# A two-layer transformer kernel: the gate products behind the last latent scores, q by ScalarE, the last expert chunks by bank, and a transpose behind the first attention step

## The chip, the core and the metric

The kernel runs on one core of one Trainium2 chip. A core has a matrix engine (TensorE, in the profile PE, with its weight loads as PEld), a vector engine (VectorE, DVE), an activation engine (ScalarE, ACT), GpSimd (POOL) and SyncE (SP), which here issues the DMAs. Each engine works through its own queue in order, and the queues meet at semaphores. Matrix products land in PSUM, which the kernel divides into eight banks; VectorE or ScalarE must read a bank before TensorE may fill it again.

The metric is the device time of one execution in microseconds (us), the median of several runs. Lower is better.

## The reference

The input is 1,024 tokens of 256 features (one sequence; B = 1). Two layers follow, each an attention and an expert stage, with a layer norm that is scaled and shifted ("modulated") ahead of each and a gated residual behind it:

```python
mod = (silu(L0_c) @ L0_wmod).reshape(1, 6, 1, -1)          # sa, ca, ga, sb, cb, gb
ga = (2 * (ga >= 0) - 1) * maximum(abs(ga), 0.25)           # gb the same
h = layernorm(x) * (1 + ca) + sa
x = x + ga * L0_attn(h)     # 16 heads with a low-rank latent (64 wide), rotary part; and a small
                            # "pattern" attention of 16 heads, 16 wide; mixed by a softmax gate
h = layernorm(x) * (1 + cb) + sb
x = x + gb * L0_ffn(h)      # 8 experts of 256: silu(h Wg) * (h Wu), down by Wd, weighted per token
mod = (silu(L1_c) @ L1_wmod).reshape(1, 6, 1, -1)
h = layernorm(x) * (1 + ca) + sa
x = x + ga * L1_attn(h)     # 16 heads, 16 wide, biases, causal, a slope per head on the key's place
h = layernorm(x) * (1 + cb) + sb
x = x + gb * L1_ffn(h)      # u + 2 shared + 16 routed experts of 176, relu, the top 4 of a sigmoid
return x
```

In the second layer's attention q = h Wq + bq, k = h Wk + bk, and the scores are q k / sqrt(16) plus slope times place, masked above the diagonal. In its expert stage the hidden units of all experts are laid side by side: 25 chunks of 128 units.

## The kernel before

**Tiling.** Tokens lie in tiles of 128 partitions, in two halves of 512 tokens (`i` = 0, 1), each half with its own `x`, `acc` and transposed features `hT`. All data are 32-bit floats. PSUM is cut into three kinds of tile by `sc_tile` and `mm_tile`: two "sc" tiles of two banks (128 x 1024), two "nn" banks and two "mm" banks (128 x 512). `mm_tile()` hands out nn and mm in turn. A tile is handed out again only after the engine that reads it is done; that is the commonest wait of TensorE here.

**Order of the work.** In most stages TensorE's order is that of the program text (`manual_schedule`); the order on VectorE, ScalarE and GpSimd is partly left to a scheduler when the kernel is built. Where the text interleaves two strands, one is a Python generator that is moved on at planned points of the other: `plan`/`side` in the second half, `at(n, ...)` in the latent attention.

**Latent attention of layer 0** (lines 860 to 1065). 128 tiles `n` of scores: 16 units `u` of eight (a head pair and a half of the tokens), `n = 8u ... 8u+7`. In iteration `n` the loop does `scores(n + 2)`: two products of 512 columns into an sc tile (L706), a row maximum on VectorE (`nmax`, L710, 128x1024), an exponential on ScalarE (`pr`, L914). Then `transposed(n)`: a block transpose of the probabilities on VectorE (`pt`, L923). Then whatever `at(n, ...)` put there: for unit `u`, `by_latent` (L938, a transpose of one over the sums) at `8u+8`, the products of probabilities and latents, `over_latents`, in two parts at `8u+9` and `8u+11` (L955, 128 small matmuls each, into four nn/mm banks, which ScalarE (L967) and VectorE (L970, eight additions) read at the end of the second part, and GpSimd multiplies at L972), and four `out_part` (L977, read by VectorE at L978) at `8u+14` to `8u+16`.

Also put there are two sets of products that belong to the next layer's modulation. `by_rows(1, 1, ...)` at `last - 12` = 116: two products of 512 columns (four matmul records, L126) into an mm/nn bank, which ScalarE copies out (L128, L131). `by_columns(1, 0, ...)` at `last - 4` = 124: eight products of one column (16 records, L111), which VectorE copies out (`modT`, L116 and L119). Here `last` = 128 is the first index behind the loop. Behind the loop, in the order of `n`: the last out parts of unit 14 (L977, at 128), the residual and layer norm of the first half on VectorE (L183, L184, L160 to L172; at 128), `over_latents(15, 0)` at 129, `by_latent(15)` and `over_latents(15, 1)` at 131, the transposes of the first half's features (`by_feature`, L196) at 132.

**Experts of layer 0** (L1191, L1169). The first pieces of the second layer are moved in between: the first half's projections of head pair 0 and the first eight score items (`firsts`).

**Attention of layer 1** (`small_attention`, lines 254 to 450). A projection gives k (`put_k`, L1232, ScalarE, with scale and bias; then DMAs that write the slope row into k, L1238) and q (`put_q`, L1225, VectorE), two instructions of 128x512 each. `step(i)` does one key tile of four heads' second scores (L337, into nn/mm banks; exponentials on ScalarE, L347) and, beside them, one or two first-score items (`first`, L299 into sc tiles, mask products L356, row maxima on VectorE, L305). Ahead of the loop stand the residual and layer norm of the second half (VectorE), the rest of the first half's projections and values (`rest`: L243, L250; values are copied out by ScalarE L67 and VectorE L69 in turn), and `by_feature(1, 0, 1)`, eight transposes (L196) with two ScalarE copies (L204). In the loop, `plan[0]` to `plan[4]` move on `parts`, the second half's projections: k and q of pair 0 after step 0, of pair 1 after step 1, two value tiles after step 2 and two after step 3. `plan[19]` starts `output` (transposes of the attention result, L463), `plan[21]` ends it.

**Experts of layer 1** (`modulated_experts`, lines 1293 to 1341). For each of the 25 chunks `c`: `hidden(c)` (L1307, ReLU on ScalarE L1308, times a gate row on VectorE L1316), then `down(c - 2)` (L1323), which adds the chunk into two accumulating banks: tokens 0 to 255 of the half in bank 0, 256 to 511 in bank 1. After the last chunk VectorE multiplies each bank by the gate (L1339), adds x (L1340), and SP sends 256 tokens to the output (L1341); bank 0 first.

Of the kernel before, what the change touches and what calls it, by code (L numbers as in the profile page):

```python
# [10 lines left out]
AF = mybir.ActivationFunctionType  # L11
ALU = mybir.AluOpType
AX = mybir.AxisListType

P = 128
T = 1024
NT = T // P
HID = 256
# [19 lines left out]
NC1 = -(-OWNED[-1][2] // P)  # L38
# [4 lines left out]
def adaln_two_layers(ctx: ExitStack, tc: tile.TileContext, a: dict, out: bass.AP):  # L43
    nc = tc.nc
# [7 lines left out]
    sc_tile = lambda: psum.tile([P, T], F32, tag="sc", name="sc")  # L52
# [51 lines left out]
    def by_columns(l, i, w, bank):  # L104

        js = ((0, 1, 2, 3), (6, 7), (8, 9))[i]
        pm = bank()
        for j in js:
            at = j * P - 512 * i
            for k in range(2):  # L110
                nc.tensor.matmul(  # L111
                    pm[:, j : j + 1], w[k][:, at : at + P], cs[:, 2 * l + k : 2 * l + k + 1],
                    start=(k == 0), stop=(k == 1),
                )
        if i < 2:
            nc.vector.tensor_copy(modT[l][:, 6 * i : 6 * i + 2], pm[:, 6 * i : 6 * i + 2])  # L116
        if i != 1:
            at = 2 + 3 * i
            nc.vector.tensor_scalar_add(modT[l][:, at : at + 2], pm[:, at : at + 2], 1.0)  # L119

    def by_rows(l, i, w, bank):

        ps = bank()
        cols = slice(0, 512) if l else slice((i - 1) * HID, i * HID)
        for k in range(2):
            nc.tensor.matmul(ps[:, cols], crep[l][:, k, :], w[k][:, cols], start=(k == 0), stop=(k == 1))  # L126
        gate = slice((i - 1) * HID, i * HID)
        nc.scalar.copy(gates_bc[l][:, gate], ps[:, gate])  # L128
        if l == 1:
            by_token[i] = base.tile([P, HID], F32, tag=f"bc{i}", name="bc")  # L130
            nc.scalar.copy(by_token[i], ps[:, (2 - i) * HID : (3 - i) * HID])  # L131
# [54 lines left out]
    def by_feature(l, which, i, double=False):  # L186

        done = which is None
        if double:
            sc = sc_tile()  # L190
            pts = [sc[:, :512], sc[:, 512:]]
        else:
            pts = [mm_tile() for _ in range(2)]
        for t in range(4):
            for k in range(2):
                nc.tensor.transpose(  # L196
                    pts[k][:, t * P : (t + 1) * P], acc[i][:, t, k * P : (k + 1) * P], ident
                )
        for k in range(2):
            if done:  # L200
                evacuate(hT[i][:, k, :], pts[k])
            else:
                s0 = 6 * which + k
                nc.scalar.activation(  # L204
                    hT[i][:, k, :], pts[k], AF.Identity,
                    bias=modT[l][:, s0 : s0 + 1], scale=modT[l][:, s0 + 2 : s0 + 3],
                )
# [279 lines left out]
    with pool("l0a") as l0, pool("mla") as ml:  # L487
# [10 lines left out]
        scale = (DN + DR) ** -0.5  # L498
# [390 lines left out]
        with pool("mla1") as m1, pool("mla2", 2) as m2:  # L889
# [96 lines left out]
            def at(n, fn, *args):  # L986
                beside.setdefault(n, []).append((fn, args))
# [44 lines left out]
            at(110, weights_of_thirds)  # L1032
            at(112, reload)
            last = 8 * len(units)
            at(last - 12, lambda: by_rows(1, 1, thirds[1], mm_tile))
            at(last - 4, lambda: by_columns(1, 0, thirds[0], mm_tile))
            at(last, residual, 0, gates_bc[0][:, :HID])
            at(last, lambda: whole(normalized(0)))
            at(last + 4, by_feature, 0, 1, 0, True)
# [182 lines left out]
    alibi = a["alibi"].rearrange("(g j) t -> j g t", j=4)  # L1222

    def put_q(dst, g, i, ps):
        nc.vector.tensor_scalar(  # L1225
            dst[:, g, i * 512 : (i + 1) * 512], ps, own4[:, g % 2 : g % 2 + 1], bias[:, 0, g : g + 1],
            ALU.mult, ALU.add,
        )

    def put_k(dst, g, i, ps):  # L1230
# [63 lines left out]
    def modulated_experts(i, tag, bank):  # L1294


        sums = [mm_tile(tag) for _ in range(2)]
        chunks = {}

        def hidden(c):  # L1300
            w = load(a["moe_w"][c].rearrange("p (b m) -> p b m", b=2))
            w1 = w[:, 0, :].rearrange("p (k m) -> p k m", k=2)
            if c % 2 == 0:
                chunks["he"] = he_tile()
            ps, he = bank[0](), chunks["he"][:, c % 2, :]
            for k in range(2):
                nc.tensor.matmul(ps, w1[:, k, :], hT[i][:, k, :], start=(k == 0), stop=(k == 1))  # L1307
            nc.scalar.activation(he, ps, AF.Relu, bias=b1[:, c : c + 1])  # L1308
            rows = [(n, r0, r1) for n, r0, r1 in OWNED if r0 < (c + 1) * P and r1 > c * P]
            if len(rows) > 1 or rows[0][0] != NE1:  # L1310
                g = row_tile()
                for n, r0, r1 in rows:
                    p0, p1 = max(r0 - c * P, 0), min(r1 - c * P, P)
                    by = gate_rows[i][n, :].partition_broadcast(p1 - p0) if n is not None else gate_rows[i][:NE1, :]
                    nc.sync.dma_start(g[p0:p1, :], by)
                nc.vector.tensor_mul(he, he, g)  # L1316
            chunks[c] = (he, w[:, 1, :])

        def down(c):
            he, w2 = chunks.pop(c)  # L1320
            for t in range(4):

                nc.tensor.matmul(  # L1323
                    sums[t // 2][:, t % 2 * HID : (t % 2 + 1) * HID], he[:, t * P : (t + 1) * P], w2,
                    start=(c == 0 and t % 2 == 0), stop=(c == NC1 - 1 and t % 2 == 1),
                )

        for c in range(NC1 + 2):
            if c < NC1:
                hidden(c)  # L1330
                yield
            if c > 1:
                down(c - 2)
                yield
        ov = out.rearrange("o (t p) d -> p (o t) d", p=P)
        for b in range(2):
            for t in (2 * b, 2 * b + 1):
                at = tmp.tile([P, HID], F32, name="at")
                nc.vector.tensor_mul(at, sums[b][:, t % 2 * HID : (t % 2 + 1) * HID], gates_bc[1][:, HID:])  # L1339
                nc.vector.tensor_add(x[i][:, t, :], x[i][:, t, :], at)  # L1340
            nc.sync.dma_start(ov[:, 4 * i + 2 * b : 4 * i + 2 * b + 2, :], x[i][:, 2 * b : 2 * b + 2, :])  # L1341
# [24 lines left out]
    with tc.manual_schedule(engines={mybir.EngineType.PE}):  # L1366
        wts = [golden(0, spare[0]), None]

        def later():
            wts[1] = golden(1)  # L1370
            gates(1, lambda: row_tile()[:, :HID])

        do = side({5: [(lambda: by_feature(0, 1, 1), None)], 8: [(later, None)]})
        for n, _ in enumerate(golden_experts(0, wts[0], True)):
            do(n)
        residual(0, gates_bc[0][:, HID:])
        whole(normalized(0))
        gated_output()

        qT, kT, v = small_tensors(l1)  # L1380
        nrm = l1.tile([P, 4, NH, 16], F32, name="nrm")
        late = [l1, [nrm, nrm]]
        firsts, step, n_steps, last_divided = small_attention(l1, qT, kT, v, True, late)
        next(firsts)
        parts = projections(0, [0], False)
        plan = {2: [(parts, 1)], 4: [(lambda: by_feature(1, 0, 0), None)]}
        for n in range(2):
            plan[6 + n] = [(parts, 1)]
        for n in range(8):
            plan[9 + 2 * n] = [(firsts, 1)]  # L1390
        do = side(plan)
        for n, _ in enumerate(golden_experts(1, wts[1], False)):
            do(n)
            if n == 20:
                rest = projections(0, [1], True)
                next(rest)
        residual(1, gates_bc[0][:, HID:])
        whole(normalized(1))
        whole(rest)
        parts = projections(1, [0, 1], True)  # L1400
        next(parts)
        by_feature(1, 0, 1)

        output = small_output(in_two(he_tile()), nrm, wo, put, 0, bv, (ones, bo))
        inputs = experts_input(0, nc.gpsimd)
        plan = {n: [(parts, 2)] for n in range(5)}
        plan[19], plan[21] = [(output, 1)], [(output, 2)]
        for n in range(4):
            plan[22 + n] = [(inputs, 1)]
        plan[26] = [(inputs, 1)]  # L1410
        plan[31] = [(inputs, 1)]
        for n in range(33, 39):
            plan[n] = [(inputs, 1)]
        plan[40] = [(inputs, 1)]
        do = side(plan)
        bank, half = [mm_tile], [None]

        def beside_experts(n):
            step(n)
            do(n)  # L1420
            if n == 37:
                singles[:] = ["mm", "mm"]
                half[0] = modulated_experts(0, "nn", bank)
            if n >= 38:
                next(half[0])

        for n in range(30):
            beside_experts(n)
# [143 lines left out]
```

## Time and profile before

| | |
|---|---|
| median of three runs | 1320.95 us (1320.94, 1320.95, 1322.4) |
| time of the profiled execution | 1324.29 us |
| its span, first to last instruction | 1322.5 us |
| mean granted TensorE clock in it | 0.996 |
| PE, PEld busy | 1284.1 us (97%), 691.8 us (52%) |
| DVE, ACT, POOL busy | 835.9 us (63%), 619.6 us (47%), 244.4 us (18%) |

Times in a profile are in us from the start of the span. A row of the timeline gives start, length, engine, source line, operation, what is written from what, and shape; in square brackets the idle time of that engine just before, and whose work ended it. The list of waits gives, for one engine, what waited for whom, with total, number and longest. The view by stretches gives the busy time of the engine in a stretch, and the clock that it was granted (1.00 is full speed). Matmul ends are modelled, and a product of 32-bit floats appears as two records.

### The profile page before, as it was taken

What the parts mean: (1) busy time and instruction counts of PE and PEld (TensorE: products, weight loads), DVE (VectorE), ACT (ScalarE), POOL (GpSimd) and SP (SyncE); (2) the same over time, 40 slices, a digit from 0 to 9 for tenths busy, and PEclk for the clock granted to TensorE, in tenths of its full rate; (3) what the DMA queues carried; (4) which work ended last, traced back from release to release, by engine and by line L of the source; (5) the groups of instructions that cost most, each with busy time, mean ns of one, the idle gap of its engine ahead of it and who ended that gap; (6) DMA issues with size and microseconds to landing.
All of it is one profiled execution on the core that took longest, in us unless ns stands there. A gap on an engine that the chain in (4) does not pass through costs nothing.

```text
span 1322.5 us, 25183 instructions
## 1 busy us (share of the span) xinstructions
PE 1284.1 (97%) x10588; PEld 691.8 (52%) x10588; DVE 835.9 (63%) x1290; ACT 619.6 (47%) x1153; POOL 244.4 (18%) x241
## 2 busy tenths in 40 slices
PE   9999999999999999999999899999989999999998
PEld 6533234324555555555555566655656454566665
DVE  4678877737787787887878875344566675152222
ACT  5366665565756657575665333111045565312121
POOL 5000000042535335252543010000000040020000
PEclk9999999999999999999999999999999999999999
DMA  9100000000000000000004022222210000325441
GB/s 285 51 0 1 1 1 1 1 1 17 10 5 6 6 5 10 2 9 2 2 1 160 2 56 71 80 80 72 65 42 10 2 2 3 112 92 162 148 157 48
DMA packets 56666, 58.82 MB, mean 44 GB/s; under 512 B 15143, under 2 KB 42280, under 8 KB 56554
## 3 DMA queue, kind: packets, MB, share of 16 engines
q1 hardware_dynamic: 56010, 57.22, 14.4%
q8 instruction: 83, 1.36, 0.4%
q14 instruction: 29, 0.24, 0.1%
q10 hardware_dynamic: 544, 0.00, 0.0%
HBM read 55.05 MB, written 1.12 MB: 42 GB/s over the span
## 4 chain that ended last, share of the span: by engine, by line
PE 89%; DVE 7%; issue 1%; POOL 1%; ACT 1%; DMA 0%; DVEq 0%; ACTq 0%; POOLq 0%
PE sc L706 17%; PE sc L299 11%; PE sc L1307 6%; PE mm L955 5%; DVE mx L305 4%; PE sc L1191 4%; PE nn L955 4%; PE nn L369 4%; PE nn L1323 3%; PE mm L1323 3%; PE mm L369 3%; PE nn L1169 2%; PE nn L1191 2%; PE mm L1169 2%; PE mm L1191 2%; PE mm L666 2%
## 5 line engine op out<-in xcount | busy, mean ns | idle before, releaser
L305 DVE TENSOR_REDUCE mx<-sc 128x2 f32<-128x1024 f32 (+3 forms) x224 | 239.6, 1106 | 51.9 <-PE sc L299 15.6
L299 PE MATMUL sc<-kT,qT 32*128 32x512 f32 (+3 forms) x896 | 204.8, 585 | 18.7 <-DVE mx L305 18.4
L914 ACT ACTIVATE pr<-sc,nmax 128x1024 f32<-128x1024 f32 x128 | 142.5, 1113 | 168.9 <-DVE nmax L710 163.0
L337 PE MATMUL nn<-q,kT 32*128 32x512 f32 (+3 forms) x384 | 189.0, 590 | 2.0 <-DVE t L626 2.0
L337 PE MATMUL mm<-q,kT 32*128 32x512 f32 (+3 forms) x384 | 187.2, 593 | 0.5 <-DVE qf L671 0.5
L923 DVE STREAM_TRANSPOSE pt<-pr 128x1024 f32<-128x1024 f32 x128 | 157.3, 1236 | 42.2 <-ACT pr L914 42.0
L710 DVE TENSOR_REDUCE nmax<-sc 128x1 f32<-128x1024 f32 x128 | 154.3, 1214 | 43.5 <-PE sc L706 41.7
L347 ACT ACTIVATE pt<-nn 128x512 f32<-128x512 f32 (+1 forms) x192 | 106.8, 556 | 62.9 <-PE mm L337 42.8
L347 ACT ACTIVATE pt<-mm 128x512 f32<-128x512 f32 (+1 forms) x192 | 106.9, 557 | 55.9 <-PE nn L337 23.4
L955 PE MATMUL mm<-pt,kv 32*64 32x256 f32 x2048 | 124.9, 382 | 2.4 <-DVE pt L923 2.4
L955 PE MATMUL nn<-pt,kv 32*64 32x256 f32 x2048 | 122.5, 382 | 0.7 <-ACT bc L942 0.7
L706 PE MATMUL sc<-kf,qf 128*128 128x512 f32 x256 | 121.1, 604 | 1.5 <-ACT pr L914 1.2
L706 PE MATMUL sc<-x,qf 128*128 128x512 f32 x256 | 121.0, 604 | 1.2 <-ACT pr L914 1.1
L299 PEld LDWEIGHTS sc<-kT,qT 32*128 32x128 f32 x896 | 65.9, 184 | 102.7 <-DVE mx L305 87.5
L1316 DVE TENSOR_TENSOR he<-he,row 128x512 f32<-128x512 f32 x46 | 31.7, 692 | 128.5 <-ACT he L1308 106.8
L635 POOL TENSOR_TENSOR t<-t,cos 128x512 f32<-128x512 f32 x32 | 40.7, 1272 | 350.3 <-PE sc L337 217.4
L955 PEld LDWEIGHTS nn<-pt,kv 32*64 32x64 f32 x2048 | 87.5, 133 | 18.2 <-DVE acc L978 6.4
L955 PEld LDWEIGHTS mm<-pt,kv 32*64 32x64 f32 x2048 | 85.0, 133 | 23.0 <-issue 5.5
L1308 ACT ACTIVATE he<-sc,b 128x512 f32<-128x512 f32 x43 | 29.5, 687 | 123.3 <-PE sc L1307 123.3
L1307 PE MATMUL sc<-hT,w 128*128 128x512 f32 x172 | 80.7, 593 | 0.0
L706 PEld LDWEIGHTS sc<-x,qf 128*128 128x128 f32 x256 | 45.6, 190 | 57.7 <-issue 51.4
L706 PEld LDWEIGHTS sc<-kf,qf 128*128 128x128 f32 x256 | 45.5, 190 | 56.7 <-issue 51.9
(382 smaller groups left out, 2117.0 us busy)
## 6 DMA issues: line engine op xcount, KB each, us to landing
w<-in_moe_w_dram SPq DMA_DIRECT2D x50, 256.0 KB
w<-in_wg_dram SPq DMA_DIRECT2D x16, 256.0 KB
w<-in_wu_dram SPq DMA_DIRECT2D x16, 256.0 KB
w<-in_wd_dram SPq DMA_DIRECT2D x16, 256.0 KB
row<-gD SPq DMA_DIRECT2D x14, 256.0 KB
x<-in_x_dram SPq DMA_DIRECT2D x4, 512.0 KB
wo<-in_o_dram SPq DMA_DIRECT2D x1, 2048.0 KB
wm<-in_wmod_dram SPq DMA_DIRECT2D x6, 256.0 KB
```

The lines of the kernel that those rows point to most:

```text
L299: nc.tensor.matmul(sc[:, i, :n], qT[r, g, qt * P : (qt + 1) * P], kT[r, g, c * 512 : c * 512 + n], start=True, stop=not diag,)
L305: nc.vector.tensor_reduce(mx[:, qi, c, 2 * pair : 2 * pair + 2], sc[:, :, :n], AX.X, ALU.max)
L337: nc.tensor.matmul(ps[:, q0:], kT[r, g, kc * P : (kc + 1) * P], state[u]["q2"][r, q0:], start=True, stop=not diag,)
L347: nc.scalar.activation(pt[:, 2 * pair + i, q0:], ps[:, q0:], AF.Exp)
L369: nc.tensor.matmul(av[PW * j : PW * (j + 1), q0:], v[:, kc, 4 * g + j, :], pt[:, j, q0:], start=(n == some[0]), stop=(n == some[-1]),)
L706: nc.tensor.matmul(sc[:, c], qfs[p, i][j][:, t * P : (t + 1) * P], kf[p % 2][j][:, c], start=True, stop=True)
L710: nc.vector.tensor_reduce(nmax, sc, AX.X, ALU.max, negate=True)
L914: nc.scalar.activation(pr, sc, AF.Exp, bias=nmax, accum_out=sums[u][:, t, j : j + 1])
L923: nc.vector.transpose(pts[u][:, :, slice(1, 3) if j else slice(0, 4, 3), 32 * t : 32 * t + 32], prs.pop(n).rearrange("p (b c k) -> p b c k ...
L955: nc.tensor.matmul(av[r][64 * c : 64 * c + 64, : 2 * P], kv32[row, b + c, :], pt[row, b // 2, 2 * c : 2 * c + 2, :].rearrange("p j q -> p ...
L1191: nc.tensor.matmul(gu[s], w[s][:, k, f * P : (f + 1) * P], hT[i][:, k, :], start=(k == 0), stop=(k == 1),)
L1307: nc.tensor.matmul(ps, w1[:, k, :], hT[i][:, k, :], start=(k == 0), stop=(k == 1))
```

## The change

Four edits, and shifts by one step that go with the last:

1. `by_rows(1, 1)` and `by_columns(1, 0)` of the latent attention are no longer issued at 116 and 124, inside the loop, but together at 128, behind the last score tiles and the last out parts of unit 14, and into one sc tile instead of nn/mm banks.
2. `put_q` of layer 1's attention is a ScalarE activation (identity with scale and bias) instead of a VectorE instruction.
3. In `modulated_experts` the products `down` of the last two chunks are ordered by bank: both chunks into bank 0, then bank 0's output, then both chunks into bank 1 and its output.
4. `by_feature(1, 0, 1)` comes after step 0 of the attention loop instead of ahead of it; the second half's projections come one step later each, and `output` starts at step 20 instead of 19.

```diff
             last = 8 * len(units)
-            at(last - 12, lambda: by_rows(1, 1, thirds[1], mm_tile))
-            at(last - 4, lambda: by_columns(1, 0, thirds[0], mm_tile))
+
+            def behind_scores():
+                sc = sc_tile()
+                by_rows(1, 1, thirds[1], lambda: sc[:, :512])
+                by_columns(1, 0, thirds[0], lambda: sc[:, 512:])
+
+            at(last, behind_scores)
             at(last, residual, 0, gates_bc[0][:, :HID])
...
     def put_q(dst, g, i, ps):
-        nc.vector.tensor_scalar(
-            dst[:, g, i * 512 : (i + 1) * 512], ps, own4[:, g % 2 : g % 2 + 1], bias[:, 0, g : g + 1],
-            ALU.mult, ALU.add,
+        nc.scalar.activation(
+            dst[:, g, i * 512 : (i + 1) * 512], ps, AF.Identity,
+            bias=bias[:, 0, g : g + 1], scale=own4[:, g % 2 : g % 2 + 1],
         )
...
-        def down(c):
-            he, w2 = chunks.pop(c)
-            for t in range(4):
+        def down(c, b):
+            he, w2 = chunks[c]
+            for t in (2 * b, 2 * b + 1):
...
-        for c in range(NC1 + 2):
-            if c < NC1:
-                hidden(c)
+        for c in range(NC1):
+            hidden(c)
+            yield
+            if c > 1:
+                for b in range(2):
+                    down(c - 2, b)
+                del chunks[c - 2]
                 yield
-            if c > 1:
-                down(c - 2)
-                yield
...
         for b in range(2):
+            for c in (NC1 - 2, NC1 - 1):
+                down(c, b)
+            yield
             for t in (2 * b, 2 * b + 1):
...
         next(parts)
-        by_feature(1, 0, 1)
...
-        plan = {n: [(parts, 2)] for n in range(5)}
-        plan[19], plan[21] = [(output, 1)], [(output, 2)]
+
+        plan = {n: [(parts, 2)] for n in range(1, 5)}
+        plan[0] = [(lambda: by_feature(1, 0, 1), None)]
+        plan[20], plan[21] = [(output, 1)], [(output, 2)]
```

No matrix product is added or removed, no DMA either. In the order of the built kernels, VectorE's queue behind unit 13's additions reads in the kernel before: maximum 118, transpose 118, maxima 119 and 120, transpose 119; in the changed one: maxima 118 and 119, transposes 118 and 119, maximum 120. Ahead of unit 15's products it reads: maxima 126 and 127, transpose 126, one L978, transpose 127, one L978, L930, two L978, `modT` (L116, L119), the residual. On ScalarE the copies L128 and L131 stand behind the exponential of tile 127. On SP the only difference is that bank 0's first output is issued one weight load earlier for the first half of the tokens.

More of the change, by code (lines that the diff above doesn't have):

```diff
@@ L1317, in hidden @@
             chunks[c] = (he, w[:, 1, :])
-        def down(c):
-            he, w2 = chunks.pop(c)
-            for t in range(4):
+        def down(c, b):
+            he, w2 = chunks[c]
+            for t in (2 * b, 2 * b + 1):
                 nc.tensor.matmul(
-                    sums[t // 2][:, t % 2 * HID : (t % 2 + 1) * HID], he[:, t * P : (t + 1) * P], w2,
+                    sums[b][:, t % 2 * HID : (t % 2 + 1) * HID], he[:, t * P : (t + 1) * P], w2,
                     start=(c == 0 and t % 2 == 0), stop=(c == NC1 - 1 and t % 2 == 1),
                 )
-        for c in range(NC1 + 2):
-            if c < NC1:
-                hidden(c)
-                yield
+        for c in range(NC1):
+            hidden(c)
+            yield
             if c > 1:
-                down(c - 2)
+                for b in range(2):
+                    down(c - 2, b)
+                del chunks[c - 2]
                 yield
```

## The prediction

> **What bounds the kernel now.** I read part 1 of the page first (two rows), then TensorE's list of waits, then stretches of 3.41 us around the longest of them, then single rows of the timeline.
>
> ```profile
> PE 1284.1 (97%) x10588; PEld 691.8 (52%) x10588; DVE 835.9 (63%) x1290; ACT 619.6 (47%) x1153; POOL 244.4 (18%) x241
> ```
>
> TensorE is busy 1284.1 of 1322.5 us, so 38 us at most can be had without taking products away, and none are. The change can win only where TensorE waits, or where its clock falls. Its waits by releaser (line waiting, line waited for, total us, times, longest):
>
> ```profile
> PE sc L299 <- DVE mx L305: 18.4, 41, 1.5
> PE mm L955 <- DVE pt L923: 2.4, 1, 2.4
> PE sc L706 <- ACT pr L914: 2.3, 2, 1.2
> ...
> PE nn L463 <- DVE nrm L389: 1.0, 1, 1.0
> PE mm L196 <- DVE v L69: 1.0, 1, 1.0
> ```
>
> By the trace the change reaches seven waits: 1.21 at 728.06 (L706), 2.38 at 755.14 (L955), 1.00 at 963.83 (L196), 1.04 at 967.00 and 1.46 at 982.24 (L299), 1.00 at 1041.67 (L463), and the end. The rest of the 18.4 on L305 lies in later steps, which keep their order. Now the clock (stretch and length, PE busy, granted clock, DMA share and rate; the other engines' columns aren't needed):
>
> ```profile
> 756.24:759.65 3.41, 2.12 (x44) 1.38 (x52) 3.38 (x7) 0.00 (x0) 0.61 (x1) 1.00 0.00 0
> 759.65:763.06 3.41, 3.41 (x73) 2.61 (x64) 3.31 (x11) 0.00 (x0) 0.00 (x0) 0.50 0.00 0
> 964.45:967.87 3.42, 2.17 (x32) 1.51 (x32) 1.50 (x3) 2.00 (x3) 0.00 (x0) 1.00 0.27 77
> ...
> 981.52:984.93 3.41, 1.75 (x52) 1.07 (x41) 3.41 (x5) 0.26 (x1) 0.00 (x0) 1.00 0.25 82
> 984.93:988.34 3.41, 3.41 (x29) 2.72 (x30) 0.79 (x3) 1.06 (x4) 0.00 (x0) 0.50 0.00 0
> ```
>
> The clock halves for one stretch of 3.41 us behind a stretch with 1.29 or 1.66 us of idle TensorE, and not behind the one with 1.24. At half clock a stretch does 1.71 us of work less. So a gap costs its length and, from about 1.3 us within one stretch, up to 1.7 more.
>
> **Part 1: the gate products go behind the last scores.** *At 720 to 748.* L126's four records (0.43 us each, 1.72) leave the place between scores 118 and 119. Scores 119 then run 721.95 to 723.77. Scores 120 need the sc tile of 118, whose maximum VectorE starts only at 723.00, behind the additions L970, and whose exponential ends at 725.43: a **new gap of 1.7**. From 725.5: scores 120 until 727.3, an L977 until 727.75, scores 121 at once (exponential 119 is over at 726.6, as VectorE now takes maximum 119 ahead of transpose 118), so the 1.21 at 728.06 goes. Scores 122 wait for exponential 120 (maximum behind transpose 119, 728.0 to 729.2; over at about 730.6): another 0.65. They start at 730.65 instead of 731.52. Carried to the next product unit this is −1.0 (ends: 0, if VectorE's later units were the pace, and −2.9 = 1.72 + 1.21, if no gap came). The new gap lies within one stretch with more than 1.3 us idle in most positions of the grid (a gap of 1.7 has at least 1.3 in one stretch in (3.41 − 1.7 + 0.8)/3.41 = 74% of them). I count the halved clock: 1.7, less some 0.3 that the 0.65 gap absorbs, +1.4 (ends 0 and 1.7).
>
> *At 748 to 764.* VectorE's rows of before:
>
> ```profile
> 750.81 1.22 DVE L710 TENSOR_REDUCE nmax<-sc 128x1 f32<-128x1024 f32 x1
> ...
> 753.45 1.23 DVE L710 TENSOR_REDUCE nmax<-sc 128x1 f32<-128x1024 f32 x1 [1.29 <-PE sc L706]
> 754.71 1.25 DVE L923 STREAM_TRANSPOSE pt<-pr 128x1024 f32<-128x1024 f32 x1
> ...
> 756.24 1.23 DVE L923 STREAM_TRANSPOSE pt<-pr 128x1024 f32<-128x1024 f32 x1
> 757.40 0.44 DVE L978 SCALAR_TENSOR_TENSOR acc<-nn,gsm,acc 128x256 f32<-128x256 f32 x1
> ```
>
> VectorE sits idle 1.29 because scores 127 stand behind the L111 products; L955 then waits 2.38 for the transposes, and its next tiles wait for the L978 that end at 758.69. Changed: scores 126 and 127 run 747.93 to 751.5; maxima 750.81 to 753.15; transpose 126 to 754.5, one L978, transpose 127 to 756.1, three L978 and L930 to 757.3. TensorE waits 0.65 for cx (the GpSimd product L972 ends at 752.18), does four L977 (1.7), L126 (1.72) and L111 (1.7), until 757.3, and starts L955 at once with its tiles free. Before it started at 757.53 but lost 1.2 to the tiles and 1.7 to the clock. So −0.1 − 1.2 − 1.7 = −3.0; I take −2.8 (ends −1.1, if the clock was not lost in the median run, and −3.4). What hides L126 and L111 here is VectorE's chain from maximum to transpose, and were it shorter they would cost their 3.4. The residual chain of VectorE (L183 at 758.72 to L172's end at 765.74) now has L116 and L119 (0.15 each) ahead of it but starts at 757.85; the transposes L196 that need it come at about 765.5, 0.6 behind its new end.
>
> By the Trainium skill (TensorE: Matmul & The Clock Gate, Why this matters for your kernels), the clock falls behind one idle window of about 3.4 us, and gaps up to about 3 us do no harm. The trace agrees on the length, 3.41, but not on the gap: it shows 0.50 behind 1.29 and 1.66 idle. By that page of the Trainium skill the new gap costs only itself: the sum would be that of the first rival below.
>
> **Parts 2 and 4: q on ScalarE, the features behind step 0.** Eight L1225 (0.8 us each; two take 1.53) leave VectorE, and as many of L1232's kind (two take 1.45) join ScalarE. TensorE's own work is unchanged, so only the waits count. (a) The rest of the first half ends 0.35 earlier: an L250 waits there for the L1225 at 961.83. (b) The 1.00 at 963.83 goes, since step 0 needs no features. (c) 1.04 at 967.00 stays about 1.0 in step 0, for its maxima still run behind the values' copies. (d) Step 1 gets about 0.4 anew: its projections need the copies L204 (0.77 each), which stand behind step 0's four exponentials on ScalarE. (e) For the 1.46 the rows are
>
> ```profile
> 980.99 1.53 DVE L1225 TENSOR_SCALAR qT<-mm,own,bias 128x512 f32<-128x512 f32 x2 [2.75 <-PE mm L243]
> 982.43 2.68 DVE L305 TENSOR_REDUCE mx<-sc 128x2 f32<-128x1024 f32 x3
> ```
>
> Three maxima of 0.9 must run between the scores and the next; without L1225 ahead they could start 1.4 earlier, but the scores end only at 981.9, so 1.46 becomes about 1.3 or less, and with it the clock loss at 984.93 may stay. (f) Step 3 gets about 0.5: a bank of q is read behind k on ScalarE, 0.7 later than before, and an L337 product wants that bank. Sum −0.35 − 1.00 + 0.4 − 0.15 + 0.5 = −0.6, with shorter maxima queues in the three other steps (two of 0.2 to 0.4 each) −1.2. Bounds: 0, if each wait comes back, and −3, if the half clock goes too. No run shows an identity with a tensor as scale for q itself; L1232, the same form for k, is the nearest row. Queued behind q on ScalarE are the exponentials of the next step, and through their banks TensorE.
>
> L463 moves behind step 20: its wait of 1.00 for nrm (VectorE's L389, ending at 1042.53) is covered by step 20's products: −0.8 (ends 0 and −1.0).
>
> **Part 3: last chunks by bank.**
>
> ```profile
> 1316.17 0.75 DVE L1339 TENSOR_TENSOR at<-mm,gbc 128x256 f32<-128x256 f32 x2 [2.90 <-PE mm L1323]
> 1316.84 0.75 DVE L1340 TENSOR_TENSOR x<-x,at 128x256 f32<-128x256 f32 x2
> 1317.51 0.74 DVE L1339 TENSOR_TENSOR at<-mm,gbc 128x256 f32<-128x256 f32 x2
> ```
>
> TensorE ends at 1316.99; bank 1's L1339 starts at 1317.51, held by bank 0's chain. Bank 0 is now done behind 16 of the last 24 records instead of 20 (0.22 each), 0.9 earlier, so its chain (1.41) ends before 1316.99: −0.5. Chunk 24's hidden row (over at 1313.26) is needed at 1314.3 at the earliest, so nothing is late. The output DMA behind it stays whole. Half 0's end lies beside other work: 0.
>
> **Sum.** −1.0 + 1.4 − 2.8 − 1.2 − 0.8 − 0.5 = −4.9. The profiled execution took 1324.29 (span 1322.5 and 1.8 around it): 1319.4. The median of the runs, 1320.95, is 3.34 below it; −4.9 there is 1316.05, which I round to **1316.0**.
>
> **Rivals.** *The new gap does not trip the clock* (its length is my walk of rows, and 0.4 less would do): −6.3, **1314.7**. The 1.24 idle without a drop speaks for it. Chance 0.27. (By the Trainium skill's rule, named above, this is the outcome.) *ScalarE gives back parts 2 and 4*: its queue per step is four exponentials, k and q (about 4.9 us against TensorE's 6.5), and copies of hT; if the waits come back under its name, the −1.2 and −0.8 are gone: **1318.0**. For it: L1232 already sits beside the exponentials that hold L337's banks. Chance 0.13. *The other sign*: if ScalarE cannot drain k, q and exponentials in a step, each of steps 1 to 3 waits for a pair of q (1.45), and each wait over 1.3 us halves the clock once (1.7): +9.5 in place of −1.2, **1326.7**. It decides once ScalarE's work per step passes 6.5 us; 4.9 speaks against. Chance 0.06. *The change does less than it says*, because the median run lost neither clock stretch (3.34 is near 2 x 1.71): without 1.7 of −2.8, and without the +1.4, −4.6: **1316.4**, within the forecast; I give both together 0.47. *More*, with the drop at 984.93 gone as well: **1314.3** down to 1313.0, chance 0.07.
>
> **Numbers.** The forecast is 1316.0, by the likeliest case. The range 1313.2 to 1318.4 takes in the rivals below 1318.3 and the bounds of part 1; the slower case is left out. A difference of 0.2% is 2.6 us, about what a measurement of this kernel can tell from no change, so faster means under 1318.3. Faster: 0.82; the same, mainly the ScalarE case with a little more lost: 0.12; slower: 0.06.
>
> **What would show it.** Right: a wait of L706 on L914 near 1.7 us at about 724 with 0.50 in the next stretch; no wait of L955 on L923, and 1.00 at 759 to 763; no wait of L196 on L69; L463's wait gone; bank 1's L1339 right behind TensorE's end. Wrong: no gap at 724 (part 1 then gains more); L337 or L243 waiting on ScalarE's L1230 or L1237 by over 1 us (parts 2 and 4 lose); L955 still late, with VectorE busy throughout.

## The result, and the profile after

| | before | after |
|---|---|---|
| median, 11 executions each | 1322.41 us | 1318.69 us |
| shortest to longest | 1320.93 to 1325.88 | 1316.66 to 1320.02 |
| profiled execution (span) | 1324.29 (1322.5) | 1319.96 (1318.2) |
| PE busy; mean granted clock | 1284.1; 0.996 | 1283.2; 0.997 |

The ratio is 0.997, with an interval of 0.9962 to 0.9979: faster by 0.3%. The forecast was 1316.0 and its range ended at 1318.4, so the direction was right, the gain too large, and the time 0.3 us outside the range.

TensorE's waits of the changed kernel (line waiting, line waited for; total, times, longest us):

```profile
PE sc L299 <- DVE mx L305: 17.8, 39, 1.3
PE sc L706 <- ACT pr L914: 3.1, 3, 1.8
...
PE sc L111 <- ACT bc L131: 0.7, 1, 0.7
PE nn L955 <- ACT bc L942: 0.7, 1, 0.7
PE mm L977 <- POOL cx L972: 0.6, 1, 0.6
```

The waits of L955 on L923, of L196 on L69 and of L463 on L389 are gone, as forecast. New are the one of 1.8 (1.83 at 723.77, forecast 1.7) and one that was not forecast: L111 waits 0.7 for L131. The two products lie in the two halves of one sc tile, and in the trace L111 starts (755.12) only when ScalarE has read the other half (L131 ends at 755.07). TensorE's rows there, the last of them the first product of L955:

```profile
752.50 1.02 PE L126 MATMUL sc<-sw,crep 128*128 128x512 f32 x2
753.36 1.02 PE L126 MATMUL sc<-t,crep 128*128 128x512 f32 x2
755.12 0.38 PE L111 MATMUL sc<-cs,sw 128*128 128x1 f32 x2 [0.74 <-ACT bc L131]
...
757.35 0.69 PE L955 MATMUL mm<-pt,kv 32*64 32x256 f32 x2
```

The clock, by stretches (length, then busy time of PE, PEld, DVE, ACT and POOL; granted clock; DMA share and rate):

```profile
722.41:725.82 3.41, 1.58 (x5) 0.54 (x4) 3.16 (x5) 1.57 (x3) 1.26 (x1) 1.00 0.02 5
725.82:729.24 3.42, 3.42 (x10) 1.69 (x10) 3.42 (x4) 0.94 (x3) 0.00 (x0) 1.00 0.00 0
753.14:756.55 3.41, 2.67 (x16) 1.62 (x14) 2.64 (x6) 0.65 (x2) 0.61 (x1) 1.00 0.00 0
756.55:759.96 3.41, 3.41 (x53) 2.47 (x60) 2.40 (x4) 0.00 (x0) 0.00 (x0) 0.50 0.00 0
759.96:763.38 3.42, 3.42 (x73) 2.17 (x64) 2.20 (x11) 0.00 (x0) 1.04 (x1) 0.50 0.03 5
```

This contradicts my price for a gap. Behind 1.83 us of idle the clock stayed at 1.00; behind only 0.74 us of idle it fell, for two stretches.

Matching each product of the two profiles in order shows where the time went: the changed kernel is 1.5 us ahead at 747, 0.2 at 757 and 0.1 at 764 (the whole lead of part 1 is lost again), 3.85 from 1100 on, and 4.3 at the end. The stretch at half clock that the profile before has at 985 (1.7 us) is absent from this profile of after, so parts 2 and 4 account for about 2.0 of the 3.75 gained between 764 and 1100. At the end, VectorE's last chain now follows TensorE's end at once, 0.5 of the gain (L1349 and L1350 are L1339 and L1340 of before):

```profile
1312.13 0.75 DVE L1350 TENSOR_TENSOR x<-x,at 128x256 f32<-128x256 f32 x2
1313.18 0.76 DVE L1349 TENSOR_TENSOR at<-mm,gbc 128x256 f32<-128x256 f32 x2 [0.30 <-PE mm L1328]
```

### The profile page after: what moved, and what is told of

Read it like the earlier page. It is cut to its first block, busy times and chain, and to the rows that moved or that the text cites. A ratio compares the mean times of both kernels' runs of the same rounds, so it can differ in the third digit from the quotient of the medians.

```text
span 1318.2 us, 25189 instructions
## 1 busy us (share of the span) xinstructions
PE 1283.2 (97%) x10588; PEld 693.6 (53%) x10588; DVE 830.6 (63%) x1282; ACT 625.0 (47%) x1161; POOL 244.3 (19%) x241
## 3 DMA queue, kind: packets, MB, share of 16 engines
q8 instruction: 83, 1.36, 0.4%
## 4 chain that ended last, share of the span: by engine, by line
PE 90%; DVE 6%; issue 1%; POOL 1%; ACT 1%; DMA 0%; DVEq 0%; ACTq 0%; POOLq 0%
PE sc L706 16%; PE sc L299 11%; PE mm L955 6%; PE sc L1312 6%; PE sc L1196 4%; DVE mx L305 4%; PE nn L369 4%; PE nn L1328 3%; PE nn L955 3%; PE mm L1328 3%; PE mm L369 3%; PE nn L1174 2%; PE nn L1196 2%; PE mm L1174 2%; PE mm L1196 2%; PE mm L666 2%
## 5 line engine op out<-in xcount | busy, mean ns | idle before, releaser
L923 DVE STREAM_TRANSPOSE pt<-pr 128x1024 f32<-128x1024 f32 x128 | 157.2, 1236 | 41.3 <-ACT pr L914 41.1
L955 PE MATMUL mm<-pt,kv 32*64 32x256 f32 x2048 | 124.9, 384 | 0.0
L955 PE MATMUL nn<-pt,kv 32*64 32x256 f32 x2048 | 123.1, 385 | 0.7 <-ACT bc L942 0.7
L955 PEld LDWEIGHTS mm<-pt,kv 32*64 32x64 f32 x2048 | 84.8, 134 | 23.6 <-issue 8.4
L955 PEld LDWEIGHTS nn<-pt,kv 32*64 32x64 f32 x2048 | 87.9, 134 | 15.0 <-issue 5.3
```

What stands on the lines that cost most here:

```text
L923: nc.vector.transpose(pts[u][:, :, slice(1, 3) if j else slice(0, 4, 3), 32 * t : 32 * t + 32], prs.pop(n).rearrange("p (b c k) -> p b c k ...
L955: nc.tensor.matmul(av[r][64 * c : 64 * c + 64, : 2 * P], kv32[row, b + c, :], pt[row, b // 2, 2 * c : 2 * c + 2, :].rearrange("p j q -> p ...
```

## The experiments

Two theories stood against each other at first. **C** (clock): the edits save what they should, and the clock takes a part back. **S** (ScalarE): part 1 earned what was forecast, and the gain is lost on ScalarE (parts 2 and 4).

**Each edit alone, on the kernel before.** Edit 1 (`e_gates`):

> Only the first edit: the gate products behind the last scores. Theory C (the clock ate part 1): products earlier by 1.5 us at 747, but L111 waits 0.7 for ScalarE's L131 and two stretches at half clock follow, so the profile shows the section over at about the same time as before (within 0.5 us), the median lies within 1 us of the kernel before, and executions without halved stretches are 1.2 to 1.6 faster. Rival S (part 1 earned its 2.8 and the gain was lost later, on ScalarE): median 2.5 to 4 us faster, with no halved stretch near 757.

Edit 2 (`e_q`):

> Only the second edit: q by ScalarE. Theory C: 0.3 to 0.8 us faster (the first half's rest ends earlier, the wait at 982 gets shorter), clock stretch at 985 there or not. Rival S: 0 to 2 us slower, with L243 or L337 waiting on ScalarE's L1230.

Edit 4 (`e_feat`, with its plan):

> Only the fourth edit: features behind step 0, projections and output one step later. Theory C: the waits at 963.8 (1.00) and 1041.7 (1.00) go, a new one of 0.3 to 0.5 in step 1: 1.2 to 1.7 us faster. Rival S: under 0.5 faster, since step 1 waits for the ScalarE copies behind the exponentials.

Edit 3 (`e_bank`):

> Only the third edit: the last two chunks by bank. Both theories: the last chain starts 0.5 us earlier, 0.4 to 0.5 us faster; nothing else moves, so the median differs by no more than the number of halved stretches lets it.

The medians tell little: ratios of 0.9995 (0.9986 to 1.0003), 1.0007 (0.9994 to 1.0021), 0.9995 (0.9986 to 1.0005) and 0.9999 (0.9987 to 1.0011). No edit alone can be told from no change. But the executions of one kernel lie in steps, and each step goes with a step in that execution's mean granted clock. Before has 59 executions in the sets run beside the experiments, with these medians by clock: 1320.80 at 0.999 (27 executions), 1322.20 at 0.998 (18), 1324.1 to 1327.4 at 0.996 to 0.994 (14). A halved stretch of 3.41 us costs 1.7 at most, and 1.71 / 1321 is 0.0013 of the mean clock. So I compare executions of equal clock (at 0.999 an execution has no halved stretch, at 0.998 one):

| kernel | clock compared | time there | before there | difference | at 0.999 or more | median of all |
|---|---|---|---|---|---|---|
| before | | | | | 27 of 59 | 1321.99 |
| after (two sets) | 0.999 | 1316.67 | 1320.80 | -4.1 | 5 of 16 | 1318.45 |
| edit 1 | 0.999 | 1319.18 | 1320.80 | -1.6 | 2 of 11 | 1321.31 |
| edit 2 | 0.999 | 1320.24 | 1320.80 | -0.6 | 1 of 12 | 1322.62 |
| edit 4 | 0.998 | 1320.75 | 1322.20 | -1.45 | 0 of 11 | 1322.00 |
| edit 3 | 0.999 | 1320.25 | 1320.80 | -0.55 | 1 of 11 | 1321.97 |
| all but edit 1 | 0.998 | 1319.89 | 1322.20 | -2.3 | 0 of 11 | 1321.04 |

At equal clock every edit pays, and the four sum to -4.2 against -4.1 for all together. S is refuted: in the trace of edit 2 no product waits for ScalarE's q, and the wait on the maxima at 981 is 1.30 instead of 1.46. The rows of edits 2 and 3 rest on one execution each, and that of edit 1 on two. The rows at 0.998 also assume that the one halved stretch cost as much in both kernels; it cost 1.4 in the kernel before and 1.7 in the changed one, so they may be off by some 0.3. The profile of edit 1 has two halved stretches in a row, as C expected, but at 272.6, a place that no edit touches, and not near 757: that part of C's expectation did not come in that execution. The last row is the changed kernel without edit 1:

> The changed kernel without its first edit. If the edits add up (shortest executions: gates -1.6, q -0.5, features -1.45, bank -0.5), the shortest is 1318.3 and half clock behind 757 comes as often as in the kernel before. If ScalarE's share takes something back in the whole, it is under 1 us below the kernel before.

Its shortest execution took 1319.87, not 1318.3. That is 0.83 under the shortest of the kernel before, and by the letter of the expectation ScalarE took something back. But each of the eleven lost at least one stretch to the clock, at equal clock its -2.3 stands against -2.6 for the sum of the three, and in its trace no product between 950 and 1050 waits for ScalarE. So ScalarE takes nothing back that could be seen beyond those 0.3.

**What sets the clock?** My prediction took idle time (theory I: from 1.3 us in a stretch). The rival, theory W: the clock follows the work that the array does in a stretch. I count a matmul record's streaming time at full clock (0.43 us for 512 columns of 32-bit floats, half of that for the mask products L356, of 16-bit floats, whose groups of 128 columns follow each other every 0.055 us) times its share of the 128 rows and of the 128 columns; an N = 1 product then counts nearly nothing, and L955's 32 x 64 tiles, four of them side by side, half. The probe puts thin products where TensorE never waits:

```
+            def thin_products():
+                pm = mm_tile()
+                for j in range(24):
+                    nc.tensor.matmul(pm[:, j : j + 1], ident, cs[:, 0:1], start=True, stop=True)
+            at(62, thin_products)
```

> The kernel before with 24 more products of one column (48 records like L111's, about 5.1 us, result unused) between the scores of iteration 62, where TensorE never waits. Theory W (the clock follows the work on the array in a stretch of 3.41 us, and falls below about 1.25 us of full-array work): no idle arises, yet at least one stretch at half clock follows in every execution, wherever the grid lies; the shortest execution is 1320.8 + 5.1 + 1.7 or more = 1327.6 at least. Theory I (the clock follows idle TensorE time, from 1.3 us in a stretch): no stretch at half clock there, the shortest execution is 1325.9.

Stretches of its profile around the products, which the trace shows from 529.26 to 536.3 without a break:

```profile
525.88:529.29 3.41, 3.41 (x13) 1.58 (x12) 3.21 (x5) 3.35 (x7) 0.25 (x2) 1.00 0.13 38
529.29:532.71 3.42, 3.42 (x33) 3.42 (x31) 2.48 (x3) 2.33 (x4) 0.51 (x1) 1.00 0.00 0
532.71:536.12 3.41, 3.41 (x18) 3.41 (x17) 0.12 (x1) 0.11 (x1) 0.00 (x0) 0.50 0.02 5
536.12:539.54 3.42, 3.42 (x6) 1.57 (x6) 0.00 (x0) 0.00 (x0) 0.00 (x0) 0.50 0.00 0
```

PE is busy in the whole of each stretch, and the clock is halved for two. The four timed executions took 1329.02 to 1331.58, none near theory I's 1325.9. A second probe keeps the streaming full and shrinks the array's share:

```
+                for _ in range(8):
+                    nc.tensor.matmul(pm[:32, :], ident[:32, :32], gates_bc[0][:32, :], start=True, stop=True)
```

> The kernel before with 8 more products of 512 columns that use only 32 x 32 of the array (16 records, about 6.9 us at 0.43 each, result unused), at the place of the first probe. They stream without a break but bring a sixteenth of full-array work. Theory W (work is streaming time times the share of rows and columns): half clock follows in every execution, the shortest is 1320.8 + 6.9 + 3.4 = 1331 or more. Rival W' (streaming alone counts, whatever the share): no half clock there, the shortest is 1327.7.

The executions took 1330.93 to 1333.4, and the profile has three halved stretches behind the 9.66 us that the products took, against 1327.7 and none by W':

```profile
530.15:533.56 3.41, 3.41 (x9) 0.84 (x8) 1.66 (x3) 2.44 (x4) 0.00 (x0) 1.00 0.00 0
533.56:536.97 3.41, 3.41 (x5) 0.69 (x4) 0.00 (x0) 0.00 (x0) 0.00 (x0) 0.50 0.00 0
```

So neither idle time nor streaming alone decides. Counted as above over the stretches of all 14 traces (the ends of the spans left out), every stretch followed by half clock holds at most 1.23 us of full-array work, and every other one at least 1.29. The first stretch of three traces (0.90 to 0.99) is no exception, though the view prints 1.00 behind it: no clock is recorded there for the first 4 to 7 us, and the products show half clock (with `a_owntile` one of L772's every 0.213 us until 6.84, and every 0.112 from 6.99 on). The figures depend on where within its record a product's work is put, as the ends are modelled: put against the modelled end, the two sides come to 1.26 and 1.29, and put right at the recorded start they overlap (1.36 and 1.30). Rows and columns are both needed. By the share of rows alone the stretch of before from 756.2 (half clock follows) holds 1.9 and that from 46.3 (full clock follows) 1.3; by the share of columns alone that from 981.5 (half) holds 4.7 or more, and that of after from 722.4 (full) 1.4. The nearest to the bound:

| trace, stretch from | idle us | full-array work us | next stretch |
|---|---|---|---|
| before, 756.2 | 1.29 | 0.98 | half |
| before, 981.5 | 1.66 | 1.18 | half |
| after, 753.1 | 0.74 | 1.19 | half |
| edit 3, 46.0 | 0.96 | 1.23 | half |
| before, 46.3 | 0.83 | 1.29 | full |
| after, 722.4 | 1.83 | 1.34 | full |
| after (second set), 752.9 | 0.74 | 1.44 | full |
| before, 964.5 | 1.24 | 1.71 | full |

The stretch behind the gap at 723.77 stayed at full clock because, by this count, the rest of it was dense score products. The last but one row is the changed kernel again, with the same wait of 0.74 and the same L111 products: there the grid of stretches lies elsewhere against the work, and the clock holds. The stretches are 3.41 us in every trace, but where they lie differs from execution to execution, which is why one kernel has several times. By the Trainium skill (TensorE: Matmul & The Clock Gate, What's actually happening) the window is free-running and does not start anew with a kernel; the shifted grids agree. Its condition for the fall, an idle window, does not: in both probes the clock falls behind stretches that the profile shows without idle.

**Repairs of part 1.** `a_owntile` gives L111 a bank of its own:

```diff
-                by_columns(1, 0, thirds[0], lambda: sc[:, 512:])
+                by_columns(1, 0, thirds[0], mm_tile)
```

> The changed kernel with the one-column products L111 in a bank of their own instead of the sc tile of L126. The 0.74 wait of L111 for ScalarE's L131 goes; L955 starts 0.7 to 1.0 earlier, when VectorE's last L978 is over. Shortest execution 1315.9 against 1316.7. Theory W: the half clock behind 757 stays in many executions, since L111 brings no work. Theory I: it goes, since no idle of 1.3 us is left there, and the median falls by over 2 us.

> The changed kernel with L111 in a bank of its own once more, beside the changed kernel itself: shortest 1315.9, and by theory W most executions without half clock, since wait, L111 and L955 no longer fall together: median 1316 to 1317.6.

> The changed kernel once more, beside the run before: shortest 1316.7, and by theory W most executions one or two halved stretches above it: median 1318.3 to 1320.

The wait is gone and L955 follows L111 at 755.9, 1.4 earlier than in the changed kernel (0.74 of it the wait, about 0.5 the half clock on L111):

```profile
755.62 0.36 PE L111 MATMUL mm<-cs,t 128*128 128x1 f32 x2
755.91 0.43 PE L955 MATMUL nn<-pt,kv 32*64 32x256 f32 x2
```

The shortest execution fell from 1316.55 to 1315.90. The medians scatter with the grid: 1315.95 and 1317.72 in the two sets (ratios to before 0.9952, 0.9939 to 0.9966; and 0.9967, 0.9955 to 0.998), beside 1318.69 and 1316.68 for the changed kernel (the second: 0.9969, 0.9956 to 0.9981). In the first set 4 of 5 executions had no halved stretch and the median was 2.7 lower: that is what I had theory I ask for, not W, so this run by itself speaks for I. In the second set the changed kernel had the lower median, against my expectation for both runs. Pooled, 6 of 10 executions have a mean clock of 0.999 or more, against 5 of 16, and the means are 1316.85 +- 0.38 and 1318.45 +- 0.35 (standard errors): 1.6 apart (+- 0.5), which is the 0.7 of the wait and, as an estimate, 0.9 of clock.

Two others use the gap at 724. `a_cols117` moves L111 there, `a_rows117` L126, and the other products stay behind the scores:

> The changed kernel with L111 at 117, in the new gap between scores 119 and 120, and L126 behind the last scores as it is. The gap of 1.83 holds L111's 1.7 for nothing; behind L126 TensorE waits 1.4 for VectorE, and L955 starts at 755.8 instead of 757.35. Shortest execution 1315.1 (1316.7 less 1.55). Theory W: the stretch with the wait keeps L126's or L955's work, half clock in some executions. Theory I: half clock behind the 1.4 wait in some, none at 724.

> The mirror of the run before: L126 (1.72 us of full-array work) at 117 in the gap, and L111 (1.7 us of one-column products) behind the last scores. The same occupancy and the same wait of 1.4 to 1.7 ahead of L955. Theory W: L111 and the wait make 3.1 to 3.4 us with almost no work, so half clock follows in every execution, often twice; the shortest is 1316.8 or more and the median 1.5 to 3 us above that of the run before. Theory I: the same times as the run before within 0.5 us.

They took 1315.43 to 1318.8 (median 1317.16; ratio 0.9959, 0.9947 to 0.9972) and 1315.18 to 1318.63 (1317.06; 0.9962, 0.9949 to 0.9974). The gap of 1.83 is gone in both. The shortest with `a_cols117` is 0.3 above its 1315.1; the shortest with `a_rows117` is 1.6 below the 1316.8 that I had W ask for. The two are equal, as I had theory I ask for, where I had W ask for 1.5 to 3 us between them. That rested on a wait of 1.4 to 1.7 ahead of L955, which came out as 0.2 and 0.3, so the two stretches without work never arose. So my reading of W missed here, and the pair by itself fits I; the probes, with half clock and no idle, decide against I.

## Why the prediction missed: point by point

- **Part 1, 720 to 748: right, a little low.** The gap came at 724 with 1.83 (1.7 forecast), the second one is 0.19 instead of 0.65, and the section gained 1.5 instead of 1.0. **The +1.4 for the clock was wrong** in this trace: the stretch holds 1.34 us of full-array work.
- **Part 1, 748 to 764: wrong.** L955 was to start at 757.3 in the time of before, 755.8 with the 1.5 taken off. VectorE had the tiles free then (its last L978 ends at 755.78), but L955 started at 757.35: 0.74 for L111 on L131, a wait that I had put at nothing, as if the halves of a tile were two tiles, about 0.5 for L111 at half clock (2.2 instead of 1.7), and 0.2 for the end of L126's last record, beside which nothing runs. Its own bank brings 755.9. The edit gives -1.6 at equal clock, where the terms without the clock say -2.1 (-1.0 and -1.1).
- **Its -1.7 for the clock: wrong.** I read the halved stretch at 759 as a property of the kernel. It belongs to an execution: 27 of 59 executions of before have none anywhere, and by their times two of the three behind 1320.95 had none, so I took 1.7 off a time in which it had not been lost. In the changed kernel L111's products, which keep PE busy and the array empty, stand beside the wait and L955's half-filled array, and its own halved stretches take the place of those that went.
- **Parts 2 and 4: right in the sum, in part by luck.** -0.6 (q) and -1.45 (features and output) at equal clock make -2.05, against -1.2 and -0.8. The 1.00 at 963.83 and L463's wait are gone, 1.04 stays, 1.46 became 1.31. The two waits that I added (0.4 in step 1, 0.5 in step 3) did not come; since the sum is right all the same, the shorter queues of maxima must have brought less than I put in, and the two errors cancel.
- **Part 3: right**, -0.55 against -0.5.
- **The failed step is the clock in the sum, and the base it stood on.** My rule, that the clock halves behind 1.3 us of idle in a stretch, is what the runs refute: full clock behind 1.83 us of idle, half clock behind none, and what decides is the work on the array. Without the clock I had -4.6, and -4.1 was measured at equal clock: 0.5 of the miss, less 0.15 by which 1320.95 lies above before's own 1320.80. For the clock I had -0.3 on that base. The median execution of the changed kernel stands 2.0 above its own time at 0.999 (1318.69 - 1316.67). That is 2.3 of the miss of 2.7. In the two profiles it shows at once: part 1 was to bring 2.4 with its clock terms (-1.0 + 1.4 - 2.8), and brought 0.1. How large the miss came out is in part chance: the second set of the same kernel has a median of 1316.68, inside the range. The rival "the new gap does not trip the clock" was right on that gap, for a reason it didn't have, and its 1314.7 is too low by the same omission. The ScalarE rival's 1318.0 is the number nearest to 1318.69, by luck: no product of parts 2 and 4 waits for ScalarE. The slower rival did not occur.

Left open: how many executions fall in which step. With edit 4, alone or with 2 and 3, no execution of 22 was free of halved stretches, while 5 of 16 were with edit 1 added. Sliding the grid through all its positions over one trace, with a bound of 1.23 to 1.29, gives a rough estimate, which moves with where a product's work is put: under 6% of the positions have no halved stretch for edit 4 alone, 10 to 20% for all but edit 1, 15 to 36% for after, 44 to 76% for the version with a bank of its own (6 of 10 executions) and 18 to 26% for before, where 46% were measured. So the bound has the order of the changed versions right and the kernel before wrong. That the distance between the weak places near 757 and 979, counted in stretches, decides it is a guess that no run here tried.

## What to carry to other kernels

Compare kernels by executions of equal mean clock first, and by medians second: here steps of 1.4 us and more hid four edits of 0.5 to 1.6 us each. When you fill a wait of TensorE, ask what the filler does on the array. By the count of work a dense product guards the clock, a one-column product only takes time, and a wait beside products of half-filled tiles is the place where the clock falls; the one pair of runs that filled the same gap with either (1317.16 and 1317.06) showed no difference. And a product into one half of a tile may wait until the other half has been read, even where the halves are two banks: the wait was 0.74, and none with a tile of its own.

## What the runs showed of the hardware

- The granted clock falls to half for a stretch of 3.41 us when the stretch before held under about 1.25 us (37%) of full-array work, counted by rows and columns in use. The nearest stretches on the two sides hold 1.23 and 1.29, closer than the modelled ends can tell apart. Idle time did not matter by itself: 1.83 us idle at full clock, 0 us idle at half.
- The clock stays at half while the work stays below that bound: the probes had two and three halved stretches in a row, the changed kernel two.
